# Attention and feed-forward on one core: side steps under a VectorE budget, squares and V's copies moved to VectorE

## The chip, the core and the metric

The kernel runs on one NeuronCore of a Trainium2 chip. Its time is the device time of one execution in microseconds. Before the change the median of three runs is 1302.34 us (1301.2 to 1303.02). The profile shows one further execution of the same kernel, with its own time.

## What is computed

The input x has 4 batches of 1024 tokens of 256 numbers. First comes attention with 16 heads of 16 on the normalised x, whose normalised output is added to x; then a gated feed-forward block, treated alike. Cut to what matters:

```python
def attn(x, Wqkv, Wout):                    # x is already normalised
    q, k, v = split_heads(x @ Wqkv.T)       # 16 heads of 16
    s = einsum("bhqd,bhkd->bhqk", q, k) / sqrt(16)
    e = exp(clip(s - max(s), -50, 50))
    out = einsum("bhqk,bhkd->bhqd", e / (sum(e) + 1e-6), v)
    return merge_heads(out) @ Wout.T

def ffn(x, w1, s1, w2, s2, h1, t1, h2, t2, w3, s3):   # ternary weights, hidden size 1024
    h = silu((x @ w1.T) * s1) * ((x @ w2.T) * s2)
    h = gelu((h @ h1.T) * t1)
    h = gelu((h @ h2.T) * t2)
    return (h @ w3.T) * s3

x = x + layernorm(attn(layernorm(x), Wqkv, Wout))
x = x + layernorm(ffn(layernorm(x), ...))
```

## The kernel before, in words

The program has two stages: attention for all four batches, up to about 627 us, and then the feed-forward block for eight half batches. The change touches the first stage only.

**Units and tiles.** Attention goes through 32 units: batch b, group g of four heads, half h of the queries (512 of them). A unit has 16 tiles. For a tile, TensorE makes scores (`exponentials`, L463, matmul at L470) into one of three PSUM buffers of two banks, and ScalarE writes their exponentials to a ring in SBUF (L471). `weigh` (L473, matmul L478) multiplies two tiles at a time with V into the accumulator `acc`. No maximum is subtracted; `rise` (L480) keeps a running maximum of the exponentials on VectorE (L487), one instruction for two tiles, which the end of a unit needs for the small term of the quotient. `vaug` is V of a group laid out in slots, copied by GpSimd (L448) from `cv`.

**Turns.** The loop at L999 goes in turns of three tiles (`TURN`). Each turn issues three score matmuls, the maxima for tiles of the turn before, one or two weighings, and then `side.take` (L630), which runs side steps. At the end of a unit (`unit_end`, L689) `acc` is copied to `o` and a chain of steps is added.

**Side steps.** Everything but scores, exponentials, maxima and weighings is a `Step` (L72) in a chain: the next batch's prologue, the division at the end of a unit (`divide`, L500), the ending of a half batch (`ending`, L544), the checks on the size of the scores (`squares` L334, `total` L342, `bound` L354, `flag` L373), the rounding of the feed-forward weights (`round_weights`, L243), and loads. A step has a gap, the turns that must pass since the step before it in its chain. A step with `tensor` uses TensorE and the single PSUM bank `misc`; at most one runs in a turn. A `heavy` one makes the turn weigh less. Chains in `first` (divisions and endings) are served ahead of those in `rest`. Near the end of a unit `take` is called with `calm`, and then only `tensor` and `quiet` steps run.

**What the steps ask of the engines.** The prologue normalises x (`Norms.gather`, `root` with a power on GpSimd at L105, `apply` at L113), transposes it (L306), and projects it: for queries and keys ScalarE writes a rounded high half from PSUM and VectorE the rest as the low half (`project` L321, L329 and L330); for V ScalarE copies PSUM to `cv` (`values` L311, L317). `squares` squares the high halves on ScalarE into `sq` (L338), which `bound` multiplies on TensorE (L360) and VectorE reduces to `norm` (L362). `divide` sends the maxima through DRAM (`top_d` and back as `folded`, both on SyncE's queue, L505 and L508), folds them (L512), transposes `o` (L517) and divides (L489 to L495). `ending` transposes the quotients (L555, copied to `oT`), projects them (`py`, L565), has ScalarE copy the result to `y`, and then takes statistics of `y`, normalises it and adds it to x (L589), all on VectorE.

**Queues.** Each engine runs its instructions in the order in which the steps issue them. SyncE's queue holds the loads, the copies that lay out queries and keys for a group (`copies`, L409, 64 KB each), and both transfers of a division. GpSimd's queue holds the copies of V, the powers, and for each of 22 weight blocks a load of 512 KB, a cast (L256) and a store. Two steps make a block: the load with a gap of one turn and the cast with a gap of three.

Of the kernel before, what the change touches and what calls it, by code (L numbers as in the profile page):

```python
# [13 lines left out]
AF = mybir.ActivationFunctionType  # L14
# [18 lines left out]
FULL = 32.0  # L33
EARLY = 256
WARM = 4
SPREAD = 32.0
# [35 lines left out]
class Step:  # L72


    def __init__(self, run, gap=0, tensor=True, heavy=False, quiet=False):
        self.run, self.gap, self.tensor, self.heavy, self.quiet = run, gap, tensor, heavy, quiet
        self.ready, self.patient = lambda: True, heavy
# [39 lines left out]
def tile_fast(ctx: ExitStack, tc: tile.TileContext, x, wqk, wv, wo, w1, w1s, w2, w2s, h1, h1s, h2, h2s, w3, w3s, out, bad):  # L117
# [62 lines left out]
    with ExitStack() as actx, ExitStack() as rctx:  # L180
# [62 lines left out]
        def round_weights(n, c):  # L243

            st = {}

            def rows(w):
                return w[c * P : (c + rows_at_once[n]) * P, :].rearrange("(i p) d -> p i d", p=P)

            def load():  # L250
                st["w"] = work.tile([P, WIDE], F32, tag="w", name="w", bufs=1)
                nc.gpsimd.dma_start(out=st["w"].rearrange("p (i d) -> p i d", i=rows_at_once[n]), in_=rows(weights[n]))

            def cast():
                st["r"] = work.tile([P, WIDE], F32R, tag="wr", name="wr", bufs=1)
                nc.gpsimd.tensor_copy(st["r"], st["w"])  # L256
                nc.gpsimd.dma_start(out=rows(rounded[n]).bitcast(F32), in_=st["r"].bitcast(F32).rearrange("p (i d) -> p i d", i=rows_at_once[n]))

            return [Step(load, 1, False), Step(cast, 3, False)]

# [11 lines left out]
        def prologue(b, space, copy):  # L272
# [38 lines left out]
            def values(t0):  # L311
                def run():
                    pv = space(f"pv_{b}_{t0}").rearrange("p (t d) -> p t d", d=D)
                    for i in range(2):
                        for c in range(DC):
                            by_slots(pv[:, i, :], st["xT"][:, c, (t0 + i) * P : (t0 + i + 1) * P], wv_sb[:, c, :], start=c == 0, stop=c == DC - 1)
                    to_scalar(cv[:, t0 : t0 + 2, :], pv)  # L317

                return run
# [14 lines left out]
            def squares(w, m, h):  # L334
                def run():
                    sq = st["sq", w, m] = work.tile([P, NQ], BF16, tag="sq", name="sq", bufs=2)
                    hi = cq[w, m, "hi"][:, h * NQ : (h + 1) * NQ].bitcast(F32)
                    nc.scalar.activation(sq, hi, AF.Square)  # L338

                return run  # L340
# [55 lines left out]

            norm = [[Step(gather(h, i), 1, False) for i in range(0, TPQ, 2)] + [Step(root(h), 0, False)] for h in range(NH)]
            xt = [[Step(apply(h, i), 1, False) for i in range(0, TPQ, 2)] + [Step(transposes(h, c), 1 if c else 2) for c in range(DC)] for h in range(NH)]
            qk = [[[Step(project(w, m, h), 1, heavy=True) for w in (1, 0)] for h in range(NH)] for m in range(DC)]
            v = [Step(values(t), 1, heavy=b > 0) for t in range(0, NT, 2)]  # L400
            flags = []
            for m in range(DC):
                flags.append([Step(total(m), 1, False)])
                for h in range(NH):
                    flags[m] += [Step(squares(w, m, h), 1, False) for w in range(2)] + [Step(bound(m, h), 1)]
            flags[-1] += [Step(gauge, 0, False), Step(flag, 1)]
            return norm, xt, qk, v, flags
# [16 lines left out]
        def few(run_all, n):  # L424


            def some(part):
                return lambda: [run() for run in part]

            return [Step(some(run_all[i : i + n]), 1, False, quiet=True) for i in range(0, len(run_all), n)]  # L430

        def stack(b, g):

            outstanding.append((b, g))

            def done():
                stacked[g % 2] = b, g
                outstanding.remove((b, g))

            steps = few([lambda copy=copy: copy(nc.sync) for w in (1, 0) for copy in copies(g, w)], 4 if g < GPT or later["qk1"] == b else 6)  # L440
            steps[0].ready = lambda: g < GPT or later["qk1"] == b
            return steps + [Step(done, 0, False, quiet=True)]

# [56 lines left out]
        def divide(g, h, o, top):  # L500
# [24 lines left out]

            return [Step(back, 2, False, quiet=True), Step(fold, 2, False), Step(run, 1)]

# [16 lines left out]
        def ending(b, h, copy):  # L544
# [41 lines left out]
            def residual(i):  # L586
# [5 lines left out]

            return (
                [Step(transposes(c), 1) for c in range(DC)] + [Step(project(t), 2, heavy=True) for t in range(0, TPQ, 2)]
                + ([Step(open_ffn, 0, False)] if (b, h) == (B - 1, NH - 1) else [])
                + [Step(gather(i), 1, False) for i in range(0, TPQ, 2)] + [Step(root, 0, False)]
                + [Step(apply(i), 1, False) for i in range(0, TPQ, 2)] + [Step(residual(i), 1, False) for i in range(0, TPQ, 2)]
            )

        class Side:  # L600


            def __init__(self):
                self.first, self.rest, self.slot = [], [], 0
                self.tired = False

# [11 lines left out]

            def next_is_heavy(self):

                for steps, at in self.first + self.rest:
                    steps = list(steps)
                    while step := self.due((steps, at), self.slot + 1, True):
                        if step.tensor:
                            return step.heavy
                        at = self.slot + 1
                        steps.pop(0)
                return False

            def take(self, calm=False):  # L630

                self.slot += 1
                free, heavy = True, False
                for chain in self.first + self.rest:
                    while (step := self.due(chain, self.slot, free)) and (step.tensor or step.quiet or not calm):
                        chain[0].pop(0)
                        chain[1] = self.slot
                        step.run()
                        free = free and not step.tensor
                        heavy = heavy or step.heavy  # L640
                self.tired = heavy

# [46 lines left out]
        def unit_end(b, g, h):  # L689
# [19 lines left out]
            if b == B - 1 and g == NG - 2:  # L709
                side.add([Step(lambda c=c: load_weights("h1", [c]), 2 if c else 0, False, quiet=True) for c in range(HC // 2)])  # L710
            if at < B:
# [9 lines left out]
            elif g == NG - 3:  # L721
                chunks = [(n, [c]) for n in ("w1", "w2") for c in range(DC)]
                loads = [Step(lambda n=n, c=c: load_weights(n, c), 2 if n == "w1" else 1, False, quiet=True) for n, c in chunks]

# [274 lines left out]
        while weighed < len(tiles):  # L999
            n = end = made  # L1000
            end += TURN
            before = weighed
            make(end)
# [19 lines left out]
            if weighed < len(tiles):  # L1023
                left = 2 * (NT - tiles[weighed][3])

                side.tired = side.tired or weighed - before >= 4
                side.take(left <= min(4, made - weighed))

# [240 lines left out]
```

## Time and profile before

| | |
|---|---|
| median of three runs | 1302.34 us |
| profiled execution: its own time, its span | 1304.9 us, 1303.1 us |
| granted TensorE clock, mean | 0.990 |
| busy: PE, PEld | 1246.2 us (96%), 771.5 us (59%) |
| busy: DVE, ACT, POOL | 700.2 us (54%), 721.6 us (55%), 119.4 us (9%) |
| last exponential ends | about 627 us |

PE is TensorE's matmuls and PEld its weight loads, DVE is VectorE, ACT is ScalarE, POOL is GpSimd, SP is SyncE; SPq and POOLq are the DMA issues in those queues. A row of a shape names the line, the engine, the operation, output and input tiles, how many there are, then busy time and mean duration, and last the idle time of the engine just ahead of them with what ended it. A row of waits says which engine waited at which line for what: microseconds in total, how often, and the longest. A row of a stretch gives its start and end, its length, and the busy time of each engine in it with the number of instructions, then the granted clock. TensorE's durations are modelled ends of pipelined matmuls, so they overlap.

### The profile page before, as it was taken

What the parts mean: (1) busy time and instruction counts of PE and PEld (TensorE: products, weight loads), DVE (VectorE), ACT (ScalarE), POOL (GpSimd) and SP (SyncE); (2) the same over time, 40 slices, a digit from 0 to 9 for tenths busy, and PEclk for the clock granted to TensorE, in tenths of its full rate; (3) what the DMA queues carried; (4) which work ended last, traced back from release to release, by engine and by line L of the source; (5) the groups of instructions that cost most, each with busy time, mean ns of one, the idle gap of its engine ahead of it and who ended that gap; (6) DMA issues with size and microseconds to landing.
All of it is one profiled execution on the core that took longest, in us unless ns stands there. A gap on an engine that the chain in (4) does not pass through costs nothing.

```text
span 1303.1 us, 21108 instructions
## 1 busy us (share of the span) xinstructions
PE 1246.2 (96%) x8104; PEld 771.5 (59%) x8104; DVE 700.2 (54%) x1578; ACT 721.6 (55%) x902; POOL 119.4 (9%) x166
## 2 busy tenths in 40 slices
PE   7998899999989999989999999999999999999995
PEld 2333333333333333323688888888888888888885
DVE  3465447763577545656653634636446464463533
ACT  3897898899888998998521413314233142231410
POOL 6221012211111000000000000000000000000000
PEclk8998999999999999999999999999999999999998
DMA  4775745666553544453230000201102011020000
GB/s 131 205 185 137 190 116 144 163 174 153 137 125 77 98 83 98 92 129 120 82 146 1 25 1 1 65 25 34 56 1 66 25 33 57 1 65 9 17 1 20
DMA packets 65678, 107.02 MB, mean 82 GB/s; under 512 B 12960, under 2 KB 39200, under 8 KB 65568
## 3 DMA queue, kind: packets, MB, share of 16 engines
q1 hardware_dynamic: 57680, 80.93, 25.4%
q0 software_dynamic: 7360, 24.12, 6.0%
q8 instruction: 66, 1.08, 0.3%
q10 hardware_dynamic: 528, 0.52, 0.2%
q14 instruction: 44, 0.36, 0.1%
HBM read 48.38 MB, written 23.59 MB: 55 GB/s over the span
## 4 chain that ended last, share of the span: by engine, by line
PE 74%; ACT 10%; DVE 8%; issue 3%; DMA 2%; POOL 1%; SPq 1%; ACTq 0%; POOLq 0%; DVEq 0%
PE ph L802 36%; PE acc L478 12%; ACT e L471 8%; PE s L470 8%; PE pz L855 4%; PE pg L802 4%; PE p L264 4%; PE py L264 2%; PE pv L264 2%; DVE sg L818 2%; PE po L517 1%; DVE ha_lo L807 1%; DVE top L487 1%; DVE st L95 1%; ACT sg L816 1%
## 5 line engine op out<-in xcount | busy, mean ns | idle before, releaser
L471 ACT ACTIVATE e<-s 128x1024 f32<-128x1024 f32 x512 | 483.8, 1043 | 43.6 <-PE s L470 36.2
L478 PE MATMUL acc<-e,vaug 128*32 128x512 f32 x2048 | 257.3, 605 | 1.0 <-POOL vaug L448 1.0
L838 ACT ACTIVATE a<-ph,h_scale 128x512 f32<-128x512 f32 x128 | 81.0, 685 | 301.4 <-PE ph L802 301.4
L470 PE MATMUL s<-sq,sk 64*128 64x512 f32 x1024 | 189.5, 447 | 22.2 <-ACT e L471 17.2
L802 PE MATMUL ph<-hb_hi,h 128*128 128x512 f32 x512 | 199.6, 390 | 0.0
L802 PE MATMUL ph<-hb_lo,h 128*128 128x512 f32 x512 | 199.4, 390 | 0.0
L470 PEld LDWEIGHTS s<-sq,sk 64*128 64x128 f32 x1024 | 87.3, 186 | 144.0 <-ACT e L471 116.5
L487 DVE TENSOR_TENSOR top<-top,e 128x512 f32<-128x512 f32 x192 | 134.0, 698 | 31.7 <-ACT e L471 26.5
L105 POOL TENSOR_TENSOR rstd<-ve,minus_half 128x4 f32<-128x4 f32 (+1 forms) x33 | 37.0, 1122 | 826.2 <-DVE ve L103 826.2
L478 PEld LDWEIGHTS acc<-e,vaug 128*32 128x32 f32 x2048 | 49.4, 109 | 106.5 <-issue 100.2
L802 PEld LDWEIGHTS ph<-hb_hi,h 128*128 128x128 f32 x512 | 96.1, 188 | 20.2
L802 PEld LDWEIGHTS ph<-hb_lo,h 128*128 128x128 f32 x512 | 96.2, 188 | 20.0
L839 DVE CAST ha_hi<-a 128x512 fp32r<-128x512 f32 x64 | 27.1, 423 | 142.7 <-ACT a L838 142.7
L802 PE MATMUL ph<-ha_hi,sq 128*128 128x512 f32 x256 | 101.9, 398 | 0.4
L802 PE MATMUL ph<-ha_lo,sq 128*128 128x512 f32 x256 | 99.9, 390 | 0.0
L802 PE MATMUL ph<-ha_lo,sk 128*128 128x512 f32 x256 | 99.8, 390 | 0.0
L802 PE MATMUL ph<-ha_hi,sk 128*128 128x512 f32 x256 | 99.8, 390 | 0.0
L816 ACT ACTIVATE sg<-pg,w_scale 128x512 f32<-128x512 f32 x64 | 43.3, 688 | 56.0 <-DVE ha_lo L807 45.6
L818 DVE SCALAR_TENSOR_TENSOR sg<-pg,w_scale,sg 128x512 f32<-128x512 f32 x64 | 47.1, 745 | 46.3 <-ACT sg L816 46.1
L839 DVE CAST hb_hi<-a 128x512 fp32r<-128x512 f32 x64 | 27.0, 422 | 71.5 <-ACT a L838 71.5
L264 PE MATMUL p<-xT,wqk_sb 128*32 128x512 f32 x512 | 61.3, 600 | 3.7 <-DVE on L495 1.4
L802 PEld LDWEIGHTS ph<-ha_hi,sq 128*128 128x128 f32 x256 | 48.1, 188 | 13.1 <-DVE sg L818 3.4
(164 smaller groups left out, 1637.3 us busy)
## 6 DMA issues: line engine op xcount, KB each, us to landing
w<-in_h_dram POOLq DMA_DIRECT2D x16, 512.0 KB, 6.4
h_r<-wr POOLq DMA_DIRECT2D x16, 512.0 KB, 4.0
x<-in_h_dram SPq DMA_DIRECT2D x32, 256.0 KB, 2.6
top_d<-top SPq DMA_DIRECT2D x30, 256.0 KB, 2.3
folded<-top_d SPq DMA_DIRECT2D x30, 256.0 KB, 3.2
sk<-ck1hi SPq DMA_DIRECT2D x64, 64.0 KB, 2.7
sk<-ck1lo SPq DMA_DIRECT2D x64, 64.0 KB, 2.7
sq<-cq1hi SPq DMA_DIRECT2D x64, 64.0 KB, 2.5
```

The source lines that it names most:

```text
L105: nc.gpsimd.tensor_tensor(rstd[:, :n], ve[:, :n], self.minus_half[:, :n], ALU.pow)
L264: nc.tensor.matmul(o[j : j + SLOT, :], w[:, j : j + SLOT], i, **flags)
L470: nc.tensor.matmul(s[:, a, :], stacks[1, g % 2, u][r, c * P : (c + 1) * P], stacks[0, g % 2, u][r, h * NQ : (h + 1) * NQ], start=True, sto ...
L471: nc.scalar.activation(pair(k)[:, u], s, AF.Exp)
L478: nc.tensor.matmul(acc[SLOT * i : SLOT * (i + 1), :], vaug[g % 2][:, c, i, :], pair(k)[:, i // 2, i % 2, :], start=c == 0, stop=c == NT - 1)
L487: nc.vector.tensor_max(top, top if c > 1 else pair(k - 2)[:, :, :, 0:P], pair(k)[:, :, :, 0:P])
L802: nc.tensor.matmul(p, homes[n][c][:, m * P : (m + 1) * P], half[:, c, :], start=c == 0 and k == 0, stop=c == len(homes[n]) - 1 and k == 1)
L816: nc.scalar.activation(sg, p[:, 0, :], AF.Silu, scale=scales["w1"][:, m : m + 1])
L818: nc.vector.scalar_tensor_tensor(sg, p[:, 1, :], scales["w2"][:, m : m + 1], sg, ALU.mult, ALU.mult)
L838: nc.scalar.activation(a, p[:, j, :], AF.Gelu, scale=scales[n][:, m : m + 1])
L839: nc.vector.tensor_copy(o[0][:, m, :], a)
L855: nc.tensor.matmul(p[t], half[:, c, t * P : (t + 1) * P], homes["w3"][c], start=c == 0 and k == 0, stop=c == HC - 1 and k == 1)
```

## The change

Five edits, all in the first stage:

- Squares (L338) and the copies of V (L317) go from ScalarE to VectorE; the first copy of V, made before the turns begin, stays on ScalarE.
- Each step that uses VectorE is given `work`, its estimate of VectorE's time in microseconds. `take` gets a `room`: 4.5, less one half of the tiles whose maxima were issued in this turn, less one where a unit starts, and at most 0.5 carried over; the work of the `tensor` step that is next is taken off. A step without `tensor` but with `work` runs only while room is left (more than 2.0 near the end of a unit, where `calm` was). `quiet` is gone.
- The norms of an ending (statistics, root, normalising, residual) are a chain of their own at the end of `rest` for all batches but the last.
- A weight block has gaps of two and four turns.
- `next_is_heavy` is split so that `take` can ask for the next `tensor` step too.

```diff
@@ -32,6 +32,7 @@
 EARLY = 256
+ROOM = 4.5
 WARM = 4
@@ -72,8 +73,8 @@
-    def __init__(self, run, gap=0, tensor=True, heavy=False, quiet=False):
-        self.run, self.gap, self.tensor, self.heavy, self.quiet = run, gap, tensor, heavy, quiet
+    def __init__(self, run, gap=0, tensor=True, heavy=False, work=0):
+        self.run, self.gap, self.tensor, self.heavy, self.work = run, gap, tensor, heavy, work
@@ -256,7 +257,7 @@
-            return [Step(load, 1, False), Step(cast, 3, False)]
+            return [Step(load, 2, False), Step(cast, 4, False)]
@@ -314,7 +315,7 @@
-                    to_scalar(cv[:, t0 : t0 + 2, :], pv)
+                    copy(cv[:, t0 : t0 + 2, :], pv)
@@ -335,7 +336,7 @@
-                    nc.scalar.activation(sq, hi, AF.Square)
+                    nc.vector.tensor_mul(sq, hi, hi)
@@ -394,16 +395,16 @@
-            norm = [[Step(gather(h, i), 1, False) for i in range(0, TPQ, 2)] + [Step(root(h), 0, False)] for h in range(NH)]
-            xt = [[Step(apply(h, i), 1, False) for i in range(0, TPQ, 2)] + [Step(transposes(h, c), 1 if c else 2) for c in range(DC)] for h in range(NH)]
-            qk = [[[Step(project(w, m, h), 1, heavy=True) for w in (1, 0)] for h in range(NH)] for m in range(DC)]
-            v = [Step(values(t), 1, heavy=b > 0) for t in range(0, NT, 2)]
+            norm = [[Step(gather(h, i), 1, False, work=1.6) for i in range(0, TPQ, 2)] + [Step(root(h), 0, False, work=0.3)] for h in range(NH)]
+            xt = [[Step(apply(h, i), 1, False, work=1.2) for i in range(0, TPQ, 2)] + [Step(transposes(h, c), 1 if c else 2, work=1) for c in range(DC)] for h in range(NH)]
+            qk = [[[Step(project(w, m, h), 1, heavy=True, work=1) for w in (1, 0)] for h in range(NH)] for m in range(DC)]
+            v = [Step(values(t), 1, heavy=b > 0, work=1) for t in range(0, NT, 2)]
...
-                flags.append([Step(total(m), 1, False)])
+                flags.append([Step(total(m), 1, False, work=1.7)])
...
-                    flags[m] += [Step(squares(w, m, h), 1, False) for w in range(2)] + [Step(bound(m, h), 1)]
-            flags[-1] += [Step(gauge, 0, False), Step(flag, 1)]
+                    flags[m] += [Step(squares(w, m, h), 1, False, work=1) for w in range(2)] + [Step(bound(m, h), 1, work=1)]
+            flags[-1] += [Step(gauge, 0, False, work=0.4), Step(flag, 1, work=2)]
@@ -427,7 +428,7 @@
-            return [Step(some(run_all[i : i + n]), 1, False, quiet=True) for i in range(0, len(run_all), n)]
+            return [Step(some(run_all[i : i + n]), 1, False) for i in range(0, len(run_all), n)]
@@ -439,7 +440,7 @@
-            return steps + [Step(done, 0, False, quiet=True)]
+            return steps + [Step(done, 0, False)]
@@ -523,7 +524,7 @@
-            return [Step(back, 2, False, quiet=True), Step(fold, 2, False), Step(run, 1)]
+            return [Step(back, 2, False), Step(fold, 2, False, work=1), Step(run, 1, work=2)]
@@ -590,18 +591,22 @@
-            return (
-                [Step(transposes(c), 1) for c in range(DC)] + [Step(project(t), 2, heavy=True) for t in range(0, TPQ, 2)]
-                + ([Step(open_ffn, 0, False)] if (b, h) == (B - 1, NH - 1) else [])
-                + [Step(gather(i), 1, False) for i in range(0, TPQ, 2)] + [Step(root, 0, False)]
-                + [Step(apply(i), 1, False) for i in range(0, TPQ, 2)] + [Step(residual(i), 1, False) for i in range(0, TPQ, 2)]
+            steps = [Step(transposes(c), 1, work=1) for c in range(DC)] + [Step(project(t), 2, heavy=True) for t in range(0, TPQ, 2)]
+            tail = (
+                [Step(gather(i), 1, False, work=1.6) for i in range(0, TPQ, 2)] + [Step(root, 0, False, work=0.3)]
+                + [Step(apply(i), 1, False, work=1.2) for i in range(0, TPQ, 2)] + [Step(residual(i), 1, False, work=1) for i in range(0, TPQ, 2)]
             )
+            if b < B - 1:
+
+                return steps + [Step(lambda: side.add(tail), 0, False)]
+            return steps + ([Step(open_ffn, 0, False)] if h == NH - 1 else []) + tail
...
                 self.first, self.rest, self.slot = [], [], 0
+                self.room = 0.0
                 self.tired = False
@@ -616,28 +621,35 @@
-            def next_is_heavy(self):
+            def next_tensor(self, slot):
...
                     steps = list(steps)
-                    while step := self.due((steps, at), self.slot + 1, True):
+                    while step := self.due((steps, at), slot, True):
                         if step.tensor:
-                            return step.heavy
-                        at = self.slot + 1
+                            return step
+                        at = slot
                         steps.pop(0)
-                return False
-
-            def take(self, calm=False):
+
+            def next_is_heavy(self):
+                step = self.next_tensor(self.slot + 1)
+                return step is not None and step.heavy
+
+            def take(self, room=math.inf, spare=0.0):
...
                 free, heavy = True, False
+                step = self.next_tensor(self.slot)
+
+                self.room = min(self.room, 0.5) + room - (step.work - step.heavy if step else 0)
                 for chain in self.first + self.rest:
-                    while (step := self.due(chain, self.slot, free)) and (step.tensor or step.quiet or not calm):
+                    while (step := self.due(chain, self.slot, free)) and (step.tensor or not step.work or self.room > spare):
                         chain[0].pop(0)
...
                         heavy = heavy or step.heavy
+                        self.room -= 0 if step.tensor else step.work
                 self.tired = heavy
@@ -707,7 +719,7 @@
-                side.add([Step(lambda c=c: load_weights("h1", [c]), 2 if c else 0, False, quiet=True) for c in range(HC // 2)])
+                side.add([Step(lambda c=c: load_weights("h1", [c]), 2 if c else 0, False) for c in range(HC // 2)])
@@ -720,7 +732,7 @@
-                loads = [Step(lambda n=n, c=c: load_weights(n, c), 2 if n == "w1" else 1, False, quiet=True) for n, c in chunks]
+                loads = [Step(lambda n=n, c=c: load_weights(n, c), 2 if n == "w1" else 1, False) for n, c in chunks]
@@ -999,7 +1011,7 @@
-            before = weighed
+            before, risen = weighed, seen
@@ -1024,7 +1036,10 @@
                 side.tired = side.tired or weighed - before >= 4
-                side.take(left <= min(4, made - weighed))
+
+                room = ROOM - (seen - risen) / 2 - (tiles[weighed][3] == 0)
+
+                side.take(room, 2.0 if left <= min(4, made - weighed) else 0.0)
```

## The prediction

> **What bounds the kernel now.** I read the page first (busy shares, slices), then stretches, then who waited for whom up to 627 us, where the last exponential ends, then the shapes of that stage, then the timeline at the stalls. After 627 us TensorE is never idle, and the two builds give it the same instructions in the same order there. Whatever the change does, it does in the first stage.
>
> ```profile
> core 0: us, PE busy (x) PEld busy (x) DVE busy (x) ACT busy (x) POOL busy (x), PEclk, DMA share, GB/s
> 27.00:627.00 600.00, 564.54 (x4729) 212.77 (x4732) 343.92 (x769) 525.40 (x600) 85.23 (x116) 0.99 0.55 134
> 359.00:375.00 16.00, 12.28 (x107) 5.07 (x107) 15.28 (x39) 13.24 (x15) 4.89 (x5) 1.00 0.43 102
> 387.00:398.00 11.00, 8.07 (x59) 3.02 (x59) 9.98 (x26) 8.92 (x10) 2.74 (x3) 1.00 0.56 120
> ```
>
> The first row is the stage. The other two are stretches after the third batch begins, in which VectorE (DVE) has 15.28 of 16 and 9.98 of 11 us to do while TensorE and ScalarE both sit idle: VectorE sets the time there.
>
> ```profile
> engine line waited for: us in total, times, longest us
> PE s L470 <- ACT e L471: 17.2, 48, 0.9
> PE po L517 <- DVE cq0lo L330: 3.6, 1, 3.6
> PE po L555 <- DVE oT L270: 2.0, 1, 2.0
> PE s L470 <- DMA sq<-cq1lo: 1.9, 1, 1.9
> PE py L264 <- DVE norm L362: 1.7, 1, 1.7
> PE pt L306 <- DVE xT L270: 1.6, 1, 1.6
> PE p L264 <- DVE on L495: 1.4, 1, 1.4
> ```
>
> TensorE's waits are few: 17.2 us for exponentials, then single long ones for VectorE (12.6 us with three smaller ones) and 3.3 us for transfers.
>
> By the row, TensorE has 600 - 564.5 = 35 us to give at most. [...] So I counted the blocks by their shortest distance from start to start in the trace: 171 triples of scores at 0.89 us (152), weighing 84 x 1.85 + 86 x 0.88 (231), query and key projections 28 x 1.83 (51), value and output projections 28 x 1.84 (52), transposes and small ones 48: 534 us of about 600. The room is some 64 us, not 35. Most of it is not to be had: from 552 us on ScalarE has nothing but exponentials, and units there still take 14.9 to 18.1 us for 16 exponentials at their distance of 0.903 us (14.4 us).
>
> **The moves off ScalarE.** These are the rows of what moves, and the nearest rows of what it becomes.
>
> ```profile
> L267 ACT ACTIVATE cv<-pv 128x512 f32<-128x512 f32 x16 | 9.6, 599 | 7.3 <-PE pv L264 6.9
> L338 ACT ACTIVATE sq<-ck0hi 128x512 bf16<-128x512 f32 x8 | 5.3, 662 | 0.0
> L270 DVE TENSOR_SCALAR o<-acc 128x512 f32<-128x512 f32 x31 | 21.4, 691 | 25.8 <-PE acc L478 25.6
> L487 DVE TENSOR_TENSOR top<-top,e 128x512 f32<-128x512 f32 x191 | 133.3, 698 | 30.5 <-ACT e L471 25.4
> ```
>
> ScalarE loses 32 squares and 15 of 16 copies of V. A lone square delays the next exponential by 0.52 us and a copy by about 1.0 (0.48 of its own, the rest waiting for its matmuls), so some 17 + 15 = 32 us leave ScalarE. That is not the gain, since TensorE mostly waits for nothing when they run. I followed each wait of the scores back along ScalarE's row to its last idle gap and took, where a square or copy lies between, the smaller of the wait and what lies there. Places (us, gain): 95 0.53, 124 0.42, 134 0.53, 163 0.26, 173 0.8, 253 0.41, 260 0.53, 263 0.4, 297 0.7, 456 0.8, 466 0.42, 533 to 549 2.1, three small ones 0.3: together 8.2 us. The largest looks like this:
>
> ```profile
> 530.73 0.62 ACT L338 ACTIVATE sq<-cq1hi 128x512 bf16<-128x512 f32 x1
> 531.25 2.84 ACT L471 ACTIVATE e<-s 128x1024 f32<-128x1024 f32 x3
> 533.96 0.65 ACT L338 ACTIVATE sq<-ck1hi 128x512 bf16<-128x512 f32 x1
> 534.48 5.62 ACT L471 ACTIVATE e<-s 128x1024 f32<-128x1024 f32 x6
> ```
>
> ScalarE runs without a gap, so each square is time. The 1.5 us at 95, 124 and 134 I don't count: SyncE's queue of copies ends late at 98 to 104 and 144 to 150 us (transfers of top_d and folded) and swallows what was won just before. **Minus 6.7 us.**
>
> **The same work on VectorE.** 47 instructions at 0.69 us (PSUM copy: row o<-acc; two SBUF inputs: row top) add 32.4 us to its 344: 376 of some 588 us, 64%. The mean is harmless; what counts is the queue. A side step's PSUM bank is reused one turn later, after at least 0.89 us of scores and 0.88 of weighing, so VectorE may come 1.77 - 0.69 = 1.1 us late before TensorE waits. Bounds of the new waits: 0 (all in idle time; VectorE idles 256 us) to 32.4 (each move lands on a late queue). The squares wait for nothing, and a copy of V waits for its matmuls as the low halves (L330) do now, with the next maxima behind it. Their rows of waits, 10 to 19 us on VectorE, cost TensorE a single wait of 3.6. I take **plus 2 us**, near the low end.
>
> [...] The rows give 599 and 691, so 15 x 0.09 = 1.4 us more work in all: small either way. [...] a maximum that met a weight cast at 393.8 us took 1.6 us instead of 0.69. POOL is busy 85 of 600 us, so 4 or 5 of 32 squares meet it, at up to 0.9 us each: 4 us of VectorE time, inside the bounds above.
>
> **The budget and the norms last.** No work goes away; statistics, normalising and residuals of batches 0 to 2 go behind everything else. I priced VectorE's order in both builds with the rows above (statistics 0.41 + 0.18, normalising 0.41, residual 0.75, reduction 1.21). Between two maxima, where some 2.6 us pass, the largest load falls from 6.4 to 5.4 us, over three such intervals from 13.2 to 9.8; the loads above 2.67 us rise from 38 to 44. It is flatter where it was worst, at the start of batch 2, and fuller elsewhere. TensorE's idle there: 2.3 us at 363, 2.0 at 371, 2.0 at 387, 1.7 at 395, together 8.0; at 215 us, 1.5, where the burst of 5.4 stays. I take 6 of 8. **Minus 6 us.** What is late next there is TensorE itself.
>
> **Six turns per weight block.** POOL doesn't follow the turns but its queue: between its copies of V at 70.7 and 112 us it casts three blocks now, two after; up to 185 us, four now and three. SyncE's order is unchanged; its waits on transfers, some 7 us up to 155 us, should fall by a third, and the two stalls that end on it with them (4.2 and 4.4 us of TensorE idle). Between 0 and 4 us; **minus 2 us.** If the last blocks came late, W1 and H1 would: the last cast stands ahead of POOL's last copy of V (564 us), and H1's loads begin about 591 us. Hidden, with some 25 us to spare.
>
> **Sum.** -6.7 + 2 - 6 - 2 = -12.7 us on a span of 1303.1 (1304.9 us for that run): span 1290.4. The median of three is 1302.3, so **1290 us**.
>
> **Rivals.** Everything pays: no new VectorE wait, and every wait of TensorE for VectorE (12.6) and transfers (3.3) goes with the 8.2: -24.1, 1278 us. For it: VectorE idles 256 us. Against: the fold behind a late transfer keeps its place in the queue, and po behind it.
> No change: gains ahead of a transfer-bound stall are swallowed, the stalls at 98 and 144 keep their size, and new VectorE waits of some 8 us eat what remains: 1302 us. For it: SyncE issues almost without pause from 72 to 103 and 112 to 155 us.
> Slower: VectorE's queue. If half of the 47 moved instructions land where it is already more than 1.1 us late, TensorE waits 47/2 x 0.69 = 16.2 us for PSUM banks, the gain at batch 2 is lost to it, and against the 8.2 won on ScalarE that is +8: 1310 us. It decides from that 1.1 us on. For it: more intervals are over 2.67 us than before.
>
> **Numbers.** Forecast 57% (1284 to 1296), all pays 21%, no change 12%, slower 10%. Range 1276 to 1303: it leaves out the lower part of the second case and the last. A measurement tells about 0.2% from no change. The first two cases are faster; of the third, a third counts as faster, 5% as same, the rest slower: 0.82, 0.05, 0.13.
>
> **What would show it.** Right: ScalarE's stage holds only exponentials, 32 high halves, 12 outputs and a few early copies; from 530 to 552 us no score waits over 0.5 us; waits of po and py on oT and norm near 363 and 371 are gone; the wait near 98 us is over 2 us still; the last exponential ends near 614. Wrong: scores or side matmuls waiting on cv or sq for more than 5 us in all, or a stage that shrinks by over 20 us.

## The result, and the profile after

The changed kernel takes 1293.8 us (median of 4 runs, 1291.56 to 1295.11) against 1302.65 us before (4 runs): a ratio of 0.9931, 95% interval 0.9915 to 0.9946, or 8.9 us less. The profiled execution took 1293.42 us, its span is 1291.6 us; the one of before had a span of 1303.1, and its own time of 1304.9 us was 2.6 above the median of the runs first shown. So the two profiles differ by 11.5 us where the medians differ by 8.9: in what follows, times of batches come from single executions, and medians and ratios decide.

The page of the changed kernel, its busy shares and the row of the granted clock:

```profile
PE 1244.4 (96%) x8104; PEld 770.0 (60%) x8104; DVE 729.1 (56%) x1625; ACT 699.2 (54%) x855; POOL 120.2 (9%) x166
...
PEclk8999899999999999999999999999999999999998
```

Before, VectorE (DVE) had 700.2 us in 1578 instructions and ScalarE (ACT) 721.6 in 902. So 47 instructions have changed engine, as the diff says. Between its two ends the clock's row has one 8 among its slices of some 32 us, the fifth, and before had one too, the fourth: the slow clock has not gone, it has moved (and lasts 6.8 us there, where before it lasted 6.8 and 3.4 in two places).

The stage of exponentials, and the two stretches behind the start of the third batch, 4 us earlier than those of before because the batch itself starts 4.2 us earlier:

```profile
core 0: us, PE busy (x) PEld busy (x) DVE busy (x) ACT busy (x) POOL busy (x), PEclk, DMA share, GB/s
27.00:615.00 588.00, 561.20 (x4722) 210.94 (x4726) 372.35 (x816) 502.85 (x554) 86.72 (x117) 0.99 0.56 137
355.00:371.00 16.00, 15.64 (x139) 6.48 (x141) 14.30 (x34) 13.61 (x16) 3.81 (x5) 1.00 0.64 150
383.00:394.00 11.00, 10.49 (x83) 3.63 (x77) 9.48 (x24) 9.46 (x12) 0.00 (x0) 1.00 0.60 143
```

The last exponential ends at 615.0 us (before 626.5): all of the 11.5 us was won in this stage, as forecast, and nothing behind it moved. Behind the start of the third batch TensorE is now busy 15.64 of 16 us and 10.49 of 11; before it had 12.28 and 8.07.

What TensorE waits for, from 27 to 620 us of the changed kernel (total, times, longest):

```profile
engine line waited for: us in total, times, longest us
PE s L471 <- ACT e L472: 13.4, 39, 0.9
PE po L518 <- DVE norm L363: 3.3, 3, 1.4
PE s L471 <- DMA sq<-cq1lo: 2.1, 1, 2.1
PE s L471 <- DMA sq<-cq0lo: 1.8, 2, 1.0
PE p L265 <- DVE on L496: 1.7, 2, 1.5
PE acc L479 <- POOL vaug L449: 1.3, 2, 1.1
PE pn L361 <- DVE sq L339: 1.0, 1, 1.0
```

Scores wait 13.4 us for exponentials instead of 17.2. The waits for oT, xT and the late low half shown before (7.2 us together) are gone, but for 0.3 us on xT. New on VectorE are 1.0 us on a square and three waits of po on norm, 3.3 us, where before had one of 0.8. Over all rows TensorE's waits for VectorE fall from 12.8 to 7.8 us. The waits of scores for transferred copies (the two DMA lines) are 3.9 us, not less than before's 3.3.

What the moved work became on VectorE, and ScalarE's row of exponentials on the page of the kernel before (L471) and on that of the changed one (L472):

```profile
L271 DVE TENSOR_SCALAR cv<-pv 128x512 f32<-128x512 f32 x15 | 10.4, 691 | 34.4 <-PE pv L265 31.0 <-PE s L471 3.4
L339 DVE TENSOR_TENSOR sq<-ck1hi 128x512 bf16<-128x512 f32 x8 | 6.2, 777 | 0.0
L339 DVE TENSOR_TENSOR sq<-cq0hi 128x512 bf16<-128x512 f32 x8 | 5.4, 680 | 0.0
```

```profile
L471 ACT ACTIVATE e<-s 128x1024 f32<-128x1024 f32 x512 | 483.8, 1043 | 43.6 <-PE s L470 36.2
L472 ACT ACTIVATE e<-s 128x1024 f32<-128x1024 f32 x512 | 482.6, 1035 | 59.4 <-PE s L471 49.7
```

A copy of V costs exactly what its nearest row said (691 ns), a square some 680 ns at the median: 33.2 us in all, where 32.4 were counted. The mean of 777 comes from one square of eight, at 362 us, that took 1.44 us; another, at 111 us, took 0.96. Both ran beside a weight cast on GpSimd. The prediction expected 4 or 5 of the 32 squares to meet one; three did, and the third (at 84 us) took 0.68. ScalarE is busy 22.4 us less, and its idle time ahead of exponentials has risen from 43.6 to 59.4 us: most of what was taken off it has become waiting for TensorE.

Where the time fell, by batch, from the first exponential of one to that of the next (the first exponential comes 0.5 us later now):

| batch | before | after | difference | forecast, by the places of its terms |
|---|---|---|---|---|
| 0 | 159.0 | 155.7 | -3.3 | -3.1 (moves -1.1, weight blocks -2) |
| 1 | 149.4 | 148.1 | -1.3 | -2.0 (moves) |
| 2 | 151.8 | 147.0 | -4.8 | -7.2 (moves -1.2, budget -6) |
| 3 | 138.9 | 136.4 | -2.5 | -2.1 (moves) |

(The +2 for new waits had no place, nor 0.3 of small moves.) Taken by itself, this table says that the prediction was right step by step. The experiments show that it was not.

### The profile page after: what moved, and what is told of

Same layout as the page of the kernel before. It is cut to its first block, busy times and chain, and to the rows that moved or that the text cites. A ratio compares the mean times of both kernels' runs of the same rounds, so it can differ in the third digit from the quotient of the medians.

```text
span 1291.6 us, 21098 instructions
## 1 busy us (share of the span) xinstructions
PE 1244.4 (96%) x8104; PEld 770.0 (60%) x8104; DVE 729.1 (56%) x1625; ACT 699.2 (54%) x855; POOL 120.2 (9%) x166
## 4 chain that ended last, share of the span: by engine, by line
PE 76%; DVE 10%; ACT 8%; issue 2%; DMA 2%; SPq 1%; ACTq 0%; POOL 0%; POOLq 0%; DVEq 0%
PE ph L814 36%; PE acc L479 13%; PE s L471 8%; ACT e L472 6%; PE pz L867 4%; PE p L265 4%; PE pg L814 3%; PE py L265 2%; PE pv L265 2%; DVE sg L830 2%; DVE top L488 2%; DVE ha_lo L819 1%; DVE st L96 1%; PE po L518 1%; ACT sg L828 1%
## 5 line engine op out<-in xcount | busy, mean ns | idle before, releaser
L472 ACT ACTIVATE e<-s 128x1024 f32<-128x1024 f32 x512 | 482.6, 1035 | 59.4 <-PE s L471 49.7
L471 PE MATMUL s<-sq,sk 64*128 64x512 f32 x1024 | 186.0, 443 | 18.2 <-ACT e L472 13.4
L471 PEld LDWEIGHTS s<-sq,sk 64*128 64x128 f32 x1024 | 86.1, 185 | 139.0 <-ACT e L472 114.6
L851 DVE CAST ha_hi<-a 128x512 fp32r<-128x512 f32 x64 | 27.1, 423 | 142.7 <-ACT a L850 142.7
```

Source lines behind the costliest of these rows:

```text
L471: nc.tensor.matmul(s[:, a, :], stacks[1, g % 2, u][r, c * P : (c + 1) * P], stacks[0, g % 2, u][r, h * NQ : (h + 1) * NQ], start=True, sto ...
L472: nc.scalar.activation(pair(k)[:, u], s, AF.Exp)
L851: nc.vector.tensor_copy(o[0][:, m, :], a)
```

## The experiments

The rival readings at this point: A, the sum as forecast (moves worth 4.7 us net, budget 6, weight blocks 2); B, the parts undo one another: SyncE's queue of copies sets the end of the first batch, so what the weight blocks' pace gives to that queue is the real gain, and the moves and the budget win little while it stands. Each experiment is compared with the kernel before on the same chip.

### Four parts, one at a time

Only the moves, on the kernel before:

```
-            nc.scalar.activation(sq, hi, AF.Square)
+            nc.vector.tensor_mul(sq, hi, hi)
-            to_scalar(cv[:, t0 : t0 + 2, :], pv)
+            copy(cv[:, t0 : t0 + 2, :], pv)
```

> The kernel before with squares and V's copies on VectorE, and nothing else of the change. The sum on record (minus 6.7 on ScalarE, plus 2 of new waits for VectorE) gives about -5 us, a ratio near 0.996. If the gain of the whole change comes from the order of VectorE's work alone, this is at or above 1.000, with the four waits at the start of batch 2 (together 8 us) as large as before or larger. If the moves carry the gain, it is near 0.993.

Measured: 0.9985 (0.9977 to 0.9994), 1301.21 us against 1303.93: a gain of 2.0 us by the ratio, of 2.7 by the medians. The waits of TensorE in this kernel:

```profile
PE s L470 <- ACT e L471: 12.7, 36, 0.9
PE po L517 <- DVE cq0lo L330: 4.5, 1, 4.5
...
PE po L555 <- DVE oT L270: 2.0, 1, 2.0
```

The waits for exponentials fall by 4.3 us, half of the 8.2 counted, and the wait of 3.6 us near 98 grows to 4.5: TensorE reaches it earlier, and what it waits for comes no earlier.

Only the budget and the norms last (the change with squares and V back on ScalarE, without their `work`, and the weight blocks' old gaps 1 and 3):

```
-            return [Step(load, 2, False), Step(cast, 4, False)]
+            return [Step(load, 1, False), Step(cast, 3, False)]
-            nc.vector.tensor_mul(sq, hi, hi)
+            nc.scalar.activation(sq, hi, AF.Square)
```

> The change without its moves and without the slower weight blocks: squares and V's copies stay on ScalarE and count as no work. The sum on record gives -6 us (ratio 0.995), with no wait over 1 us of TensorE on VectorE in the first 60 us of batch 2. If the moves carry the gain, about 0.999.

Measured: 0.9994 (0.9983 to 1.0004), 1302.57 us: no gain that can be told from none. Yet at the places that the prediction named, this kernel has:

```profile
core 0: us, PE busy (x) PEld busy (x) DVE busy (x) ACT busy (x) POOL busy (x), PEclk, DMA share, GB/s
359.00:375.00 16.00, 15.70 (x139) 6.56 (x135) 12.20 (x31) 14.23 (x16) 1.65 (x2) 1.00 0.41 84
387.00:398.00 11.00, 10.50 (x85) 3.46 (x77) 10.06 (x26) 9.89 (x11) 0.00 (x0) 1.00 0.34 59
```

TensorE is busy 15.70 and 10.50 us where it had 12.28 and 8.07: the idle time there is gone, and the third batch takes 146.7 us instead of 151.8. What gives this back in the median execution no trace shows: the profiled one took 1299.91 us, 2.7 less than the median of its 22 executions (1296.0 to 1307.0, the widest spread of all these kernels). In it the first batch is 1.6 us longer than before (160.6 us), with a wait of 3.8 us at 141 and half clock for 6.8 us behind it, and the other three are 6.7 us shorter. Over the 22 executions the slower ones have the lower granted clock (mean 0.985 to 0.993, correlation -0.79), so slow stretches behind stalls are the likely place; that is not shown.

The change with the weight blocks at their old pace:

```
-            return [Step(load, 2, False), Step(cast, 4, False)]
+            return [Step(load, 1, False), Step(cast, 3, False)]
```

> The kernel after with weight blocks of four turns as before. The sum on record gives the slower blocks 2 us, so this is about 2 us above the kernel after (ratio to before near 0.9945). If the pace of the weights has no part, it equals the kernel after (0.993).

Measured: 0.9962 (0.9948 to 0.9976), 1298.33 us. The first batch takes 162.1 us instead of the change's 155.7; batches 1 to 3 (147.9, 146.7, 136.4) stay as they were within 0.3.

The change with the norms in their old place for every batch:

```
-            if b < B - 1:
-                return steps + [Step(lambda: side.add(tail), 0, False)]
-            return steps + ([Step(open_ffn, 0, False)] if h == NH - 1 else []) + tail
+            return steps + ([Step(open_ffn, 0, False)] if (b, h) == (B - 1, NH - 1) else []) + tail
```

> The kernel after with the norms of an ending in the ending's own chain, ahead of the prologue, but under the budget. If the budget is what flattens VectorE's queue, this is the kernel after within 1 us. If it takes norms last, some 5 us of the gain are lost (ratio near 0.997) and the waits for oT and norm at the start of batch 2 are back.

Measured: 0.9913 (0.9897 to 0.993), 1291.42 us. The interval overlaps that of the change (0.9915 to 0.9946): that the norms come last brings nothing that can be seen; whether it costs some 2 us stays open.

### The weight blocks' pace alone, and the moves beside it

The kernel before with gaps 2 and 4 in place of 1 and 3, then the same with the moves, then the change without the moves:

```
-            return [Step(load, 1, False), Step(cast, 3, False)]
+            return [Step(load, 2, False), Step(cast, 4, False)]
```

> The kernel before with weight blocks of six turns and nothing else. Theory now: the first batch ends on transfers, and the pace of the weights is what sets it (first batch 162.1 us with quick blocks and 155.7 with slow ones in the kernel after), so this gains 3 to 5 us, all in the first batch, with the waits near 98 and 144 us smaller. Rival: the slower blocks only mend what the budget does to GpSimd's steps (it lets them run near the end of a unit, where they were held back), and here they gain under 1 us.

> The scheduler of before with the moves and the slower blocks, without budget and without norms last. If the budget has a part of its own, this stays 3 to 5 us above the kernel after with norms in the ending's chain (ratio near 0.995 against 0.991), with the four waits at the start of batch 2 in place, about 7 us. If moves and weights carry everything, it is near 0.991.

> The kernel after with squares and V's copies back on ScalarE, not counted as work. The moves are worth the difference to the kernel after: 2 us by the run of the moves alone (ratio near 0.9945), 4.7 us by the sum on record (0.9967), and the waits of scores on exponentials rise from 13 to 17 us or more.

Measured: the pace alone 0.9947 (0.9933 to 0.996), 1297.33 us against 1303.85: 6.5 us from two numbers in one line. With the moves 0.9925 (0.9912 to 0.9939), about 3 us more; the two intervals just overlap, the executions (1291.6 to 1296.0 with the moves, 1296.8 to 1298.3 without) do not. The change without the moves 0.9923 (0.9909 to 0.9936): the same as the whole change. A falls. B holds in the main: the weight blocks' pace is the largest gain, and the other parts win little. That SyncE's queue alone is the reason does not hold, as will be seen.

The two stalls of the kernel before, in stretches:

```profile
core 0: us, PE busy (x) PEld busy (x) DVE busy (x) ACT busy (x) POOL busy (x), PEclk, DMA share, GB/s
98.00:104.00 6.00, 3.25 (x27) 0.91 (x22) 0.72 (x2) 4.08 (x5) 0.00 (x0) 0.95 0.56 139
104.00:109.00 5.00, 4.18 (x19) 2.12 (x21) 4.43 (x11) 2.00 (x3) 0.00 (x0) 0.50 0.01 3
145.00:148.00 3.00, 0.85 (x3) 0.51 (x4) 2.11 (x6) 1.02 (x1) 0.00 (x0) 0.97 0.34 55
148.00:152.00 4.00, 4.00 (x23) 1.04 (x21) 0.14 (x1) 1.94 (x2) 0.00 (x0) 0.60 0.68 163
```

and the same neighbourhoods of the kernel with the slower pace alone:

```profile
core 0: us, PE busy (x) PEld busy (x) DVE busy (x) ACT busy (x) POOL busy (x), PEclk, DMA share, GB/s
97.00:105.00 8.00, 6.27 (x53) 2.25 (x47) 4.32 (x9) 6.09 (x7) 0.00 (x0) 1.00 0.48 107
105.00:109.00 4.00, 4.00 (x22) 1.34 (x18) 3.59 (x11) 3.04 (x4) 0.00 (x0) 0.57 0.02 4
140.00:150.00 10.00, 10.00 (x99) 4.60 (x101) 6.19 (x18) 9.03 (x11) 0.92 (x2) 1.00 0.41 93
```

Before, each stall is followed by a stretch in which TensorE looks busy and is not fast: granted clock 0.50 and 0.60, 19 matmuls in 5 us. With the slower pace the first stall is halved: TensorE waits 1.7 us instead of 3.6, and the half clock behind it lasts 3.4 us instead of 6.8. The second stall is gone: the last stretch is full (10.00 of 10) at clock 1.00, with 99 matmuls in 10 us; before had 26 in 7.

The transfers behind it, 60 to 150 us, before:

```profile
q0 software_dynamic: 1728, 6.29, 23.3%
```

and with the slower pace alone:

```profile
q0 software_dynamic: 1296, 4.72, 15.6%
```

This is GpSimd's queue, which carries the weights: 6.29 MB fall to 4.72. SyncE's copies in the same stretch pass beside it, and a read of folded (256 KB) lands in 2.8 us at the median instead of 4.9. Under one scheduler the first batch grows with these bytes: 4.72 MB 151.0 us and 6.29 (before) 159.0 under the old one, 5.23 (the change) 155.7 and 7.34 (the change at the old pace) 162.1 under the budget. But the bytes are not all: the change without the moves has 4.78 MB, hardly more than 4.72, and takes 155.5 us. There the last copy of cq1lo leaves SyncE 114.1 us after the first exponential, with the slower pace alone after 111.8. Why SyncE comes later under the budget stays open.

### Where the change stalls, and its queues

In the change the first stall is mostly gone, and the second comes about 4 us earlier. TensorE in the changed kernel, in order of time (start, length, instruction, the idle time before it and what ended it):

```profile
140.62 0.50 PE L471 MATMUL s<-sq,sk 64*128 64x512 f32 x2
143.25 1.91 PE L471 MATMUL s<-sq,sk 64*128 64x512 f32 x4 [2.13 <-DMA sq<-cq1lo]
145.09 3.64 PE L479 MATMUL acc<-e,vaug 128*32 128x512 f32 x16
```

and SyncE's own sequence ahead of it:

```profile
134.08 0.51 SPq L509 DMA_DIRECT2D folded<-top_d  x1
134.64 0.45 SPq L200 DMA_DIRECT2D w_scale<-in_w1s_dram  x1
135.14 3.52 SPq L419 DMA_DIRECT2D sq<-cq1hi  x4
138.70 0.58 SPq L200 DMA_DIRECT2D w_scale<-in_w2s_dram  x1
139.33 2.64 SPq L419 DMA_DIRECT2D sq<-cq1lo  x4
142.01 0.57 SPq L200 DMA_DIRECT2D h_scale<-in_h1s_dram  x1
```

SyncE issues without a pause, 0.4 to 0.9 us each, and the last of the four copies of cq1lo leaves at 142.0. TensorE's two scores of 140.62 are followed by 2.13 us of nothing, and the 16 weighing matmuls then take 3.64 us: from one group of four to the next 0.85 us pass at half clock, 0.43 otherwise. Between the loads that the unit waits for stand scales and other loads that nobody needs yet. Two kernels take them, or the weights, away. First, the change with these loads (wo in 16 pieces, four scales, w3s: some 21 issues) on GpSimd's queue; x stays on SyncE's, though the expectation counts it in:

```
-                return lambda: nc.sync.dma_start(out=out, in_=in_)
+                return lambda: nc.gpsimd.dma_start(out=out, in_=in_)
```

> The kernel after with the loads of x, of the output weights and of the scales on GpSimd's queue in place of SyncE's. If the stalls near 100 and 141 us come from SyncE's queue being full of issues of 0.5 to 0.6 us, taking some 35 of them away ends both (1.4 + 5.6 us), and the kernel gains 4 to 6 us on the kernel after (ratio near 0.989). If they come from the transfers themselves, it stays at 0.993.

Measured: 0.9884 (0.9868 to 0.9901), 1287.99 us. The first batch takes 149.3 us, the others as in the change (147.7, 146.9, 136.4), and in the stretch of the stall this kernel shows

```profile
139.00:150.00 11.00, 10.71 (x104) 4.33 (x104) 5.38 (x14) 8.04 (x9) 1.35 (x3) 1.00 0.54 115
```

where the changed kernel shows

```profile
139.00:150.00 11.00, 8.01 (x41) 3.28 (x39) 5.16 (x15) 4.44 (x5) 0.00 (x0) 0.69 0.59 126
```

with 41 matmuls at clock 0.69 instead of 104 at 1.00. The weights are not slower for it (ten of their transfers leave from 60 to 150 us, nine in the change), so it is the issues taken from SyncE that count here. Second, the change with the weight blocks 45 turns later, in five turns each:

```
+            side.add([Step(lambda: None, 45, False)] + [s for k in blocks for s in round_weights(*k)])
-            return [Step(load, 2, False), Step(cast, 4, False)]
+            return [Step(load, 2, False), Step(cast, 3, False)]
```

> The kernel after with the weight blocks begun 45 turns later and then in five turns each, so that none falls in the first batch. If transfers of the weights are what holds the first batch, its 155.7 us fall to 150 or less and the whole to about 1288 us (ratio 0.989), unless the later batches, whose copies then meet more weight blocks, give it back. If SyncE's queue alone holds it, the first batch stays at 155 us and the ratio at 0.993.

Measured: 0.9889 (0.9872 to 0.9906), 1289.02 us: the first batch 147.4, but the last 138.9 (136.4 in the change). There the late weights leave their mark: from 535 to 548 us TensorE has 10.56 of 13 us, at a clock of 0.87, with a wait of 1.5 us for a copy of cq1lo. Either way of relieving the queue is worth 5 to 6 us on top of the change.

### The other two parts, once the stalls are out of the way

Both reliefs together with the norms inline; the same with squares and V on ScalarE; and the same with the old scheduler instead of the budget:

> Moves and budget of the kernel after, the norms in the ending's own chain, late weight blocks, and the loads of x, output weights and scales on GpSimd's queue. No stall on transfers should be left in the first batch (about 147 us) and no half clock behind one; the sum of the single gains on the kernel after (2.3 for the chain, 5.8 for the queue) gives about 1285.5 us, ratio 0.9865.

> The kernel of the run before this one in this job (late weights, loads on GpSimd's queue), with squares and V's copies back on ScalarE. Without stalls on transfers to swallow it, the moves should be worth what the waits of scores on exponentials show, 4 to 6 us: this is 4 to 6 us above that kernel. If the moves are worth nothing anywhere, both are equal.

> The scheduler of before (no budget, norms in the ending's chain) with the moves, late weight blocks and the loads on GpSimd's queue. The budget is worth the difference to inline_late_rest_pool: 5 to 6 us by the third batch alone (151.5 against 145.3), less what it costs in the first. If both are equal, the budget gives nothing.

Measured: 0.9879 (0.9861 to 0.9896), 1287.89 us; without the moves 0.994 (0.9926 to 0.9954), 1294.98; without the budget 0.9909 (0.9894 to 0.9923), 1291.58. So here the moves are worth 7.1 us and the budget 3.7, by medians. (Of the 7.1, the profiled executions show 5.7 in the four batches and 1.2 ahead of the first exponential, where the moves change nothing. The intervals with and without the budget just touch, but the executions, 1285.5 to 1288.3 and 1290.1 to 1294.5, do not overlap. By batch the budget wins 4.7 us in the third and 3.3 in the fourth and loses 2.1 in the first.) The reliefs do not add up (1287.89 against 1287.99 for the loads alone on GpSimd's queue). These two are the fastest kernels of the study, both ahead of the change.

The waits for exponentials without the moves:

```profile
PE s L471 <- ACT e L472: 19.7, 54, 0.9
```

and with them:

```profile
PE s L471 <- ACT e L472: 12.9, 37, 0.9
```

They differ by 6.8 us, and the batches by 5.7: with no stall behind it, the time gives most of what these rows show. In the change itself the same two numbers are 13.4 with the moves and 19.4 without, and the time is the same. For the budget, the start of the third batch with it,

```profile
345.00:362.00 17.00, 16.71 (x151) 6.66 (x147) 16.11 (x39) 15.44 (x18) 4.81 (x6) 1.00 0.58 140
```

and without it:

```profile
345.00:362.00 17.00, 13.07 (x115) 5.33 (x117) 16.32 (x42) 12.02 (x13) 3.19 (x4) 1.00 0.41 91
```

VectorE is equally full in both (16.11 and 16.32 of 17 us). With the budget TensorE gets through 151 matmuls in that stretch, without it 115: what fills VectorE under the budget delays TensorE less.

## Why the prediction was right, and where it was wrong

The forecast span was 1290.4 us and the profiled one 1291.6; by medians 1290 was forecast and 1293.8 came. The total is near in part by luck: the weight blocks were priced too low, the moves and the budget too high.

**Weight blocks: the mis-sized term.** "Between 0 and 4 us; minus 2 us." Alone this part is worth 6.5 us, the largest gain of any single part. The mechanism was named rightly in outline (SyncE's copies wait for transfers, and with fewer weights they wait less: by the rows from 60 to 150 us SyncE waits 4.2 us for transfers before and 0.8 us with the slower pace alone). The failing step is "should fall by a third, and the two stalls that end on it with them". A stall is the difference of two nearly equal times, the copies' landing and TensorE's arrival; so a few us less on one side can take far more than a third of it: the first fell from 3.6 to 1.7 us, the second went whole. And its price is more than its wait. The trace of before has half clock for 6.8 us from 103.4 and for 3.4 us from 147.8, right behind the two stalls; in the change a wait of 2.1 us at 141 and 6.8 us of half clock cost 5.6 us by the distance between turns. The prediction's 4.2 and 4.4 us are counted from start to start; by the rows TensorE is idle 3.6 and 3.0 us there, and in the first the rest is slow work already, which went unnamed. How long a wait must be is not shown: in the change one of 2.1 us, behind some 1.2 us of small work and a wait of 0.85 us before that, was enough for half clock from 142.7 us. And the length of a wait does not decide alone. At the start of the third batch TensorE waits 2.0 us for oT, with the same instructions around the wait, in the kernel before (until 367.0 us) and with the slower pace alone (until 359.8). Behind it they show, in this order:

```profile
368.00:372.00 4.00, 4.00 (x36) 1.37 (x34) 3.90 (x8) 3.69 (x4) 1.72 (x2) 1.00 0.34 135
361.00:365.00 4.00, 4.00 (x22) 0.74 (x18) 3.90 (x10) 2.84 (x3) 0.00 (x0) 0.57 0.02 4
```

Full clock follows the one, half clock for 3.4 us the other. What sets it off was not tried apart, so its price can be counted behind a stall but not foretold from the wait.

**The moves: right about the rows, wrong about what stands behind them.** "Minus 6.7 us", with 2 back for new waits. The waits of scores fall by 4.3 us alone and by 6.0 or 6.8 under the budget. But what the time gives depends on what stands behind: 2 to 3 us alone (0.9985), about 3 with the slower pace, nothing measurable within the change, 7.1 with SyncE's queue relieved. The prediction left out 1.5 us at 95, 124 and 134 as swallowed by SyncE's queue; the swallowing itself was right, and too small. Two rows of the change without the moves, for comparison with those of the change above:

```profile
PE s L471 <- ACT e L472: 19.4, 54, 0.9
PE po L518 <- DVE norm L363: 0.7, 1, 0.7
```

All waits of TensorE from 27 to 620 us come to 25.8 us without the moves and to 26.4 with them: 6.0 less for exponentials, but 5.3 more for VectorE (7.8 against 2.5), 1.0 more for transfers and 0.3 for GpSimd. In the first batch (155.5 us without the moves, 155.7 with them) 3.1 us are won on exponentials. New waits on VectorE take 2.6 of them back (on a square at 98 us, on norm at 103 and 139), and waits for transferred copies another 1.0, while the copies still end at 142. In the other three batches of those two kernels the moves win 1.3 us in total (149.1, 146.7, 137.0 against 148.1, 147.0, 136.4). With SyncE relieved and the norms inline they win 3.6 us there, and 2.1 in the first batch. The difference in batches 1 to 3 is about that of one unit, from 239 to 260 us, which holds the ending's statistics: 20.7 us in the change and 17.7 without the moves, but 18.3 in the change with the norms inline (which pays in the unit from 200 us, 20.6 instead of 19.3). In that unit the change has these waits of TensorE,

```profile
PE p L265 <- DVE on L496: 1.5, 1, 1.5
PE po L518 <- DVE norm L363: 1.0, 1, 1.0
```

and neither of them is there without the moves. It seems that the statistics that were pushed last then meet the moved squares in VectorE's queue. That fits the sizes; it was not tried by itself, since the only run with the norms inline in the change does not tell its time from the change's.

**The budget: right in mechanism, only half in the sum.** "I take 6 of 8." The third batch gains 5.1 us with the budget alone and 4.8 in the change, with the waits for oT and xT gone at the places named. (Its 8.0 us are counted from start to start; by the rows of the two stretches TensorE idles 3.7 and 2.9 us there, 6.7 together.) Not foreseen was that the first batch loses: at the slower pace it takes 151.0 us with the old scheduler and 155.5 or 155.7 with the budget. "What is late next there is TensorE itself" was argued for the third batch, where it holds; in the first it is SyncE's copies, which come later under the budget, for a reason that stays open. So the budget alone is worth 0 (0.9994), and 3.7 us with the stalls out of the way.

**New waits on VectorE.** "Plus 2" was right with SyncE's queue relieved and the norms inline (2.5 us: 6.7 with the moves, 4.2 without), and too small in the change (5.3). All waits of TensorE for VectorE still fall, from 12.8 before to 7.8, since the budget takes others away; the bound of 32 us was never near. The rival "slower" (moved work late in VectorE's queue, +8) is refuted by these rows, and by the fact that the moves measurably lose in no kernel. "All pays" is refuted too. "No change" had named both things that befell the moves: a stall that swallows what is won ahead of it, and new waits on VectorE that eat the rest. It was wrong in that the stalls would keep their size, which the weight blocks' pace changed.

Of the things to look for, the end of the last exponential (615.0 for 614), ScalarE's contents, the vanished waits on oT and norm near 363 and 371, and the scores from 530 to 552 us (0.42 us at most) were right; the last tells nothing, since before had no wait over 0.5 us there either. One was wrong: the wait near 98 us is 1.0 and 1.4 us in two turns instead of over 2 (the slower pace shortened it, and the larger stall is now at 141). The 64 us of room are 66 by the prediction's own sum; nothing rests on them.

## What to carry to other kernels

Ask which queue ends each stage before adding up waits. In the first batch it was SyncE's, at 0.4 to 0.9 us an issue: a gain ahead of it was largely swallowed (the moves gave 2 to 3 us alone and 7.1 with that queue relieved), and a gain on it was worth more than its share (6.29 MB of weights cut to 4.72 halved the first stall and removed the second, 6.5 us in all, where 2 were forecast). Price a stall of TensorE with the slow clock behind it: in the kernel before, half clock for 6.8 us came with a wait of 3.6. And test each part in the context of the others: here the moves were worth some 2, 3, 0 and 7 us in four contexts, and two reliefs of 5 to 6 us each did not add.

## What was not expected of the hardware

Half clock set in during or soon after waits of TensorE: in the kernel before with those of 3.6 and 1.9 us (for 6.8 us from 103.4 and for 3.4 us from 147.8), in the change with one of 2.1 us (for 6.8 us from 142.7). One and the same wait of 2.0 us brought it with the slower pace alone (clock 0.57 from 361 to 365 us) and not in the kernel before (1.00 from 368 to 372 us). From one group of four weighing matmuls to the next 0.85 us passed at half clock instead of 0.43, while the busy rows show TensorE as full (4.00 of 4 us from 148 to 152 us before, at a clock of 0.60). Two of the three squares that ran beside a weight cast on GpSimd took 0.96 and 1.44 us instead of 0.68.
